# A kernel of conditional layer norms: boundary tokens in half tiles with gathered pair rows, and a sort with one number per token

## The chip, the cores and the metric

The kernel runs on one core of one Trainium2 chip. The metric is the device time of one execution in microseconds (us). Three executions before the change took 1043.15, 1043.70 and 1040.04 us; their median, 1043.15 us, is the time before.

## The reference

Every token has a row x of 512 floats (16 batches of 512 tokens, 8192 tokens) and three indices: a pathway (0 to 499), a compartment c (0 to 4, used for the "cp" and "tm" tables) and a mask m (0 or 1 here; the table "ms" has 3 rows).

```
h = _ln(_ln(x, pw_g[pw], pw_b[pw]), cp_g[c], cp_b[c])
t = _ln(x, tm_g[c], tm_b[c])
s = _ln(x, ms_g[m], ms_b[m])
m_, n_, r_ = x + (a small two-layer network of each batch's condition, with layer norm)   # one row per batch
cat = concatenate(w0*h, w1*t, w2*m_, w3*n_, w4*r_, w5*s)                # 3072 wide
y = _ln(silu(cat @ int_W1 + b1) @ int_W2 + b2, g, b)
out = x + y
```

`w` is a softmax of six numbers, and `_ln(x, g, b)` is (x - mean) * rsqrt(var + 1e-5) * g + b. All is float32. A layer norm's row times g is linear in the normalised row, so t and s together are norm(x) * (w1 * tm_g[c] * W1_t + w5 * ms_g[m] * W1_s) plus a row that depends on (c, m) alone. There are 15 pairs (c, m).

## The kernel before

**Tiles.** The kernel sorts the tokens by pair, so that nearly every tile of 128 sorted tokens has one pair, its primary pair. 64 tiles make 16 windows (`sts`, w = 0 to 15) of four tiles. For a window, x rows are gathered by token (`gather_x`, POOL), their sums taken (`x_sums`, ACT), and three transposed operands made: X (x itself), V (the norm, zero for tokens whose pair isn't the primary one) and H (the pathway and compartment norms). A transposed operand comes about in two steps: DVE turns 32 x 32 blocks (`turn`, L156) into a tile `rot`, and four DMAs issued by SP (`spread_row`, L164) carry a row of it into a tile `cat`, from which TensorE loads its weights. A row of `cat` needs all four gathers of its window, since the turned blocks are interleaved. There is one `rot` and one `cat` tile for each of X, V, H and Z.

Each tile has four products of four chunks of 128: X with wx_ (w2, w3, w4 times their blocks of W1), V with a matrix built for the tile's pair (`s_part` on ACT, `build` on DVE, L190 and L196), H with wh_, and the second layer's Z with w2. The condition networks' part of the first layer and all biases come as one gathered row for each token (`rows_2` in DRAM, `gather_add`).

**Boundary tokens.** A tile in which the sorted list goes from one pair to the next also holds tokens of other pairs. They get their V part apart: for each of the 14 later pairs, the 128 tokens from the tile position where it begins are one extra tile. Four windows e0 to e3 (`ext`) hold them. Their x rows are gathered, normed (`norm_v`) and turned, and for each pair k a matrix is built: `pair_s` (ACT, L597) scales ws by the ms row, `pair` (DVE, L805) adds wt times the tm row. `extra` (PE, L811) is the product, `extra_add` and `extra_end` add a gathered bias row, and `extra_out` writes the 128 rows to rows_2.

**The sort.** Before that, prefix sums of the 15 pairs give each of 8192 tokens its position: row (0 to 127) and tile column (0 to 63). For each of 64 steps (128 tokens, one on each partition) DVE or POOL builds a one-hot row matrix (L563), and DVE (L572) or ACT (L567, L569) builds a matrix with two numbers, the token and its pair with its pathway, at the token's column. A product per step (L574), summed in PSUM, puts them in place. Then the tables of tokens, pathways, compartments and primary pairs follow, by small transposing products (`swap`, L603).

**Order.** Each engine runs its instructions in the order of the program. From window 2 on, a fixed step function writes that order. Before it, the string ORDER names every piece ("gx.e0.1", "pa.4", "lX.1.0") in the order in which it is issued, across engines; a piece in that string is one helper call, and the dictionary `pieces` names the function. All DMAs of SP are issued in one queue, and gathers on POOL's. The first window's products are lX.0.*, lV.0.*, lH.0.*.

Of the kernel before, what the change touches and what calls it, by code (L numbers as in the profile page):

```python
# [8 lines left out]
F32 = mybir.dt.float32  # L9
# [5 lines left out]
P = 128  # L15
# [4 lines left out]
ORDER = """  # L20
    gx.e0.0 gx.e0.1 gx.e0.2 xs.0.0 gx.e0.3 xs.0.2 gx.e1.0 gx.e1.1 xs.0.1 gx.e1.2 xs.0.3 gx.e1.3 pwi xs.e0.0 gh.0.0
    cs cv br2 xe.0 prim cg xs.e0.3 lX.0.0 xp.0 scl cp xm.0 sp.0.0 pk gh.0.1 cn bd.0.0 ct lX.0.1 nv.0.0 lw nv.0.1
    gh.0.2 xs.e0.1 tv.0.0 tv.0.1 nv.0.2 ca lX.0.2 nv.0.3 tv.0.2 sp.0.1 tv.0.3 bd.0.1 sV.0.0 xn.0.0 lX.0.3 xs.e0.2
    f1.0.0 sV.0.1 xn.0.1 xa fp.0.0 cm xe.e0 f1.0.1 sV.0.2 ps.0 xp.e0 xm.e0 fm.0.0 fp.0.1 lV.0.0 sV.0.3 cr fn.0.0
    fm.0.1 f2.0.0 sp.0.2 bd.0.2 gh.0.3 lV.0.1 nv.e0.0 nv.e0.1 tv.e0.0 sp.0.3 gx.e2.0 tv.e0.1 bd.0.3 gx.e2.1 rp.0
    nv.e0.2 nv.e0.3 gx.e2.2 fn.0.1 tv.e0.2 rp.1 xn.0.2 gx.e2.3 tv.e0.3 rc.0 f1.0.2 xs.e1.2 ro.0 lV.0.2 sV.e0.0 rc.1
    f2.0.1 fp.0.2 xs.e1.0 pa.1 xs.e1.1 ro.1 lV.0.3 sV.e0.2 xs.e1.3 fm.0.2 pa.2 fn.0.2 ea.1 xn.0.3 sV.e0.3 ea.2
    f1.0.3 ex.2 xs.e2.2 sV.e0.1 xe.e1 f2.0.2 fp.0.3 xp.e1 fm.0.3 fn.0.3 xm.e1 f2.0.3 nv.e1.0 ea.3 nv.e1.2 ea.4
    tv.e1.0 xs.e2.0 sH.0.0 pa.4 ex.1 gx.e3.0 nv.e1.1 xs.e2.1 gx.e3.1 sH.0.1 tv.e1.1 gx.e3.2 xs.e2.3 ee.1 tv.e1.2
    eo.1 pa.3 nv.e1.3 sH.0.2 ex.3 gx.e3.3 tv.e1.3 sH.0.3 xe.e2 ee.2 xp.e2 lH.0.0 ee.3 ea.5 xm.e2 nv.e2.0 eo.2  # L30
    nv.e2.1 sV.e1.0 gx.1.0 tv.e2.0 tv.e2.1 nv.e2.2 gx.1.1 nv.e2.3 tv.e2.2 ps.1 tv.e2.3 sV.e1.1 gx.1.2 pa.5 gx.1.3
    xs.e3.0 ex.4 sV.e1.2 ea.6 xs.e3.1 pa.6 eo.3 xs.e3.2 ex.5 sV.e2.0 ee.4 xs.e3.3 sV.e2.1 ex.6 gh.1.0 ar pa.7 ea.7
    sV.e1.3 ee.5 xe.e3 pa.8 xp.e3 lH.0.1 sV.e2.2 ee.6 eo.6 ex.8 eo.4 xs.1.0 xs.1.1 xs.1.3 xm.e3 nv.e3.0 nv.e3.1
    tv.e3.0 tv.e3.1 nv.e3.2 eo.5 gh.1.1 gx.2.0 gx.2.1 nv.e3.3 tv.e3.2 sV.e2.3 tv.e3.3 gx.2.2 ex.7 sV.e3.0 ea.8 pa.9
    ea.9 sV.e3.1 lH.0.2 ee.7 eo.7 xs.1.2 ps.2 gx.2.3 xe.1 pa.10 xp.1 sV.e3.2 wm ea.10 ex.10 tx.1.0 tx.1.1 sV.e3.3
    gh.1.2 wl.1 tx.1.2 wl.2 tx.1.3 wl.3 ex.9 xm.1 pa.12 nv.1.0 wl.4 sX.1.0 ee.8 lH.0.3 ee.9 eo.8 pa.11 ea.11 sX.1.2
    ex.11 sX.1.3 ee.10 eo.9 sX.1.1 wl.0 nv.1.1 pa.13 ex.12 tv.1.0 nv.1.2 pa.14 eo.10 ea.12 ex.13 ee.11 tv.1.1 sp.1.0
    eo.11 tv.1.2 bd.1.0 ex.14 ea.13 nv.1.3 sp.1.1 tv.1.3 ea.14 lX.1.0 sV.1.1 ee.12 ee.13 xn.1.0 eo.12 eo.13 ee.14
    lX.1.1 eo.14 sV.1.2 lX.1.2 sV.1.3 ga.0.3 ga.0.0 bd.1.1 sV.1.0 lX.1.3 ga.0.1 f1.1.0 ga.0.2 xn.1.1 xn.1.3 f1.1.1
    ha.0.3 fp.1.0 lV.1.1 hs.0.3 ha.0.0 sh.0.0 fm.1.0 hs.0.0 fp.1.1 fn.1.0 tz.0.0 ha.0.1 sh.0.1 hs.0.1 lV.1.0 ha.0.2  # L40
    sh.0.2 tz.0.1 hs.0.2 tz.0.2 sh.0.3 sp.1.2 tz.0.3 f2.1.0 ga.1.0 sZ.0.1 bd.1.2 sp.1.3 ga.1.1 lV.1.2 sZ.0.2 gh.1.3
    xn.1.2 f1.1.2 sZ.0.0 ga.1.2 l2.0.1 fp.1.2 sZ.0.3 fm.1.1 bd.1.3 fn.1.1 ga.1.3 l2.0.2 f2.1.1 fm.1.2 f1.1.3 gh.2.0
    fn.1.2 l2.0.0 xs.2.0 f2.1.2 xs.2.1 fp.1.3 gh.2.1 fm.1.3 fn.1.3 xs.2.2 f2.1.3 lV.1.3 la.0.0 sH.1.0 xs.2.3 lq.0.0
    tx.2.0 tx.2.1 xe.2 tx.2.2 xp.2 sH.1.1 sp.2.0 la.0.1 l2.0.3 tx.2.3 la.0.2 xm.2 lq.0.1 gh.2.2 bd.2.0 sH.1.2 lq.0.2
    lH.1.0 xn.2.0 xn.2.1 sH.1.3 sh.1.1 sh.1.0 f1.2.0 nv.2.0 nv.2.1 sp.2.1 tv.2.0 lH.1.1 fp.2.0 sX.2.0 tv.2.1 la.0.3
    fm.2.0 f1.2.1 nv.2.2 nv.2.3 sX.2.1 lq.0.3 tv.2.2 fp.2.1 fn.2.0 tv.2.3 lv.0 f2.2.0 lp.0 sX.2.2 ha.1.0 gh.2.3
    hs.1.0 sX.2.3 lH.1.2 lb.0.0 fm.2.1 ha.1.1 fn.2.1 hs.1.1 sh.1.2 f2.2.1 po.0.0 sV.2.0 lH.1.3 tz.1.0 lb.0.1 gx.3.0
    sV.2.1 sh.1.3 sV.2.2 tz.1.1 sV.2.3 ha.1.2 lb.0.2 hs.1.2 po.0.1 gx.3.1
"""
# [3 lines left out]
def kernel(ctx: ExitStack, tc: tile.TileContext, a: dict, out: bass.AP):  # L53

# [339 lines left out]
    for k, nm in enumerate(("idx_c", "idx_m", "idx_pw")):  # L394
        nc.sync.dma_start(idx[:, k, :], a[nm])
# [6 lines left out]
    nc.sync.dma_start(ws, w1_block(5))  # L402
    nc.sync.dma_start(wt, w1_block(1))
    mx = prep.tile([P, 1], F32, name="mx")
    nc.vector.tensor_reduce(mx, aw, AX.X, ALU.max)
    nmx = prep.tile([P, 1], F32, name="nmx")
    nc.vector.tensor_scalar_mul(nmx, mx, -1.0)
    ex = prep.tile([P, 6], F32, name="ex")
    nc.scalar.activation(ex, aw, AF.Exp, bias=nmx)
    stT, w1s = [], []  # L410
    at = 0
    for nm in ("mem", "noi", "res"):
        k = a[nm + "T"].shape[0]
        kk = min(k, P)
        n = k // kk
        t = prep.tile([kk, n, B], F32, name="stT" + nm)
        nc.scalar.dma_start(t, a[nm + "T"].rearrange("(c p) b -> p c b", p=kk))
        stT.append(t)
        t = xbs[2][:kk, at : at + n, :]
        at += n  # L420
        nc.scalar.dma_start(t, a[nm + "_W1"].rearrange("(c p) f -> p c f", p=kk))
        w1s.append(t)
    b1c = prep.tile([P, 4, NC], F32, name="b1c")
    nc.scalar.dma_start(b1c, a["b1c"])
    vr = gp.tile([P, D], F32, tag="cp", name="vr")[:9]
    nc.scalar.dma_start(vr, a["vecs"][:9])
    rb2 = scratch(0, D)
    for s in range(3):
        nc.scalar.dma_start(rb2[s * L : (s + 1) * L], a["vecs"][3 * s].partition_broadcast(L))
    w2s = [xbs[1], xbs[0], w2]  # L430
    for t, nm in zip(w2s, ("mem", "noi", "res")):
        nc.sync.dma_start(t, a[nm + "_W2"].rearrange("(c p) f -> p c f", p=P))
    tabs = scratch(0, 3, NC, L)
    nc.vector.memset(tabs, 0.0)
    for k, (nm, lo, hi) in enumerate((("tm_bT", 0, NR5), ("ms_bT", NR5, NR), ("cp_bT", 0, NR5))):
        nc.sync.dma_start(tabs[:, k, :, lo:hi], a[nm].rearrange("(c p) r -> p c r", p=P))
    w1x = [yb, flat_cat("H", "w1x1"), flat_rot("H", "w1x2")]
# [661 lines left out]
```

## Time and profile before

| what | us |
|---|---|
| median of three runs | 1043.15 |
| the profiled execution: its own time | 1036.91 |
| the profiled execution: its span | 1034.9 |
| PE busy | 987.2 (95% of the span) |
| DVE busy | 876.2 (85%) |
| ACT busy | 572.7 (55%) |
| POOL busy | 570.4 (55%) |
| PE share of the chain that ended last | 82% |

The profile is one execution, taken apart by a hardware profiler; the span runs from the first instruction to the last. PE is TensorE, PEld its weight loads, DVE the vector engine, ACT the scalar engine, POOL GpSimd, SP the engine that only issues DMAs. A float32 product of one chunk of 128 is recorded as two matmuls. The 40-slice table gives each engine's busy share in tenths for slices of 25.9 us. A group row gives a line, engine, operation, output <- input, number; then busy us and mean ns of one; then the idle time of the engine in front of these instructions and what ended it. The TensorE clock granted was 0.988 of full on the mean; four short stretches between 58 and 213 us ran at half.

### The profile page before, as it was taken

What the parts mean: (1) busy time and instruction counts of PE and PEld (TensorE: products, weight loads), DVE (VectorE), ACT (ScalarE), POOL (GpSimd) and SP (SyncE); (2) the same over time, 40 slices, a digit from 0 to 9 for tenths busy, and PEclk for the clock granted to TensorE, in tenths of its full rate; (3) what the DMA queues carried; (4) which work ended last, traced back from release to release, by engine and by line L of the source; (5) the groups of instructions that cost most, each with busy time, mean ns of one, the idle gap of its engine ahead of it and who ended that gap; (6) DMA issues with size and microseconds to landing.
All of it is one profiled execution on the core that took longest, in us unless ns stands there. A gap on an engine that the chain in (4) does not pass through costs nothing.

```text
span 1034.9 us, 11013 instructions
## 1 busy us (share of the span) xinstructions
PE 987.2 (95%) x2523; PEld 447.5 (43%) x2523; DVE 876.2 (85%) x1577; ACT 572.7 (55%) x1153; POOL 570.4 (55%) x573
## 2 busy tenths in 40 slices
PE   5979799899899999999999999999999999999996
PEld 5634244343344444444444444444444444444442
DVE  7978898998889898888888888888898988888844
ACT  3698694483746473646464554647364746474311
POOL 4764661646556564737464646555565647374413
PEclk9989999999999999999999999999999999999998
DMA  9585797566767675857666676767676758677412
GB/s 281 202 264 160 225 287 222 163 178 190 198 195 201 172 224 158 231 161 212 175 195 181 194 191 187 190 198 197 193 200 174 221 155 231 163 215 179 135 51 92
DMA packets 95655, 197.66 MB, mean 191 GB/s; under 512 B 26290, under 2 KB 26290, under 8 KB 95592
## 3 DMA queue, kind: packets, MB, share of 16 engines
q0 software_dynamic: 32096, 108.55, 35.9%
q1 hardware_dynamic: 62230, 87.44, 30.3%
q10 hardware_dynamic: 1266, 0.99, 0.3%
q8 instruction: 21, 0.34, 0.1%
q14 instruction: 42, 0.34, 0.1%
HBM read 104.14 MB, written 21.44 MB: 121 GB/s over the span
## 4 chain that ended last, share of the span: by engine, by line
PE 82%; DVE 5%; DMA 4%; ACT 3%; issue 3%; SPq 1%; POOL 1%; POOLq 0%; DVEq 0%; ACTq 0%
PE p L305 57%; PE p L324 19%; PE pe L811 3%; PE pn L574 1%; SPq L164 1%; DMA xbs<-in_mem_W 1%; DMA out<-yb,tok 1%; PE ph L549 1%; DMA adde<-rows,i_addx 1%; DMA cH<-rH 1%; DVE vs L196 1%; DMA xbs<-in_x,tok_x 1%; DVE pw L289 0%; ACT vs L190 0%; DVE vs L805 0%
## 5 line engine op out<-in xcount | busy, mean ns | idle before, releaser
L305 PE MATMUL p<-vs,cV 128*128 128x512 f32 x504 | 228.4, 597 | 6.7 <-DVE vs L196 6.7
L324 PE MATMUL p<-w,cZ 128*128 128x512 f32 x512 | 228.9, 592 | 0.0
L305 PE MATMUL p<-wx__82,cX 128*128 128x512 f32 x512 | 225.2, 597 | 3.1 <-DVE add L309 2.1
L305 PE MATMUL p<-wh__83,cH 128*128 128x512 f32 x512 | 222.8, 592 | 0.0
L196 DVE SCALAR_TENSOR_TENSOR vs<-wt,sct,vs 128x512 f32<-128x512 f32 x252 | 206.3, 878 | 0.0
L190 ACT ACTIVATE vs<-ws,scs 128x512 f32<-128x512 f32 x252 | 160.7, 707 | 2.6 <-PE pe L811 2.1
L269 POOL TENSOR_TENSOR rsh<-veh,mhalf 128x1 f32<-128x1 f32 x64 | 45.9, 717 | 199.8 <-DVE veh L265 191.1
L305 PEld LDWEIGHTS p<-wx__82,cX 128*128 128x128 f32 x512 | 97.9, 192 | 126.6 <-issue 118.9
L305 PEld LDWEIGHTS p<-vs,cV 128*128 128x128 f32 x504 | 95.5, 191 | 130.9 <-issue 92.3
L324 PEld LDWEIGHTS p<-w,cZ 128*128 128x128 f32 x512 | 97.3, 190 | 122.5 <-issue 122.2
L305 PEld LDWEIGHTS p<-wh__83,cH 128*128 128x128 f32 x512 | 97.3, 190 | 122.5 <-issue 122.2
L276 ACT ACTIVATE pw<-pw,nmh,rsh 128x512 f32<-128x512 f32 x64 | 51.8, 810 | 128.0 <-DVE nmh L147 128.0
L312 ACT ACTIVATE add<-add 128x512 f32<-128x512 f32 x64 | 40.3, 630 | 146.8 <-DVE add L309 141.9
L358 POOL DMA_INDIRECT out<-yb,tok x64 | 68.2, 1066 | 63.8 <-DVE yb L353 26.9
L332 ACT ACTIVATE junk<-yb 128x512 f32<-128x512 f32 x64 | 40.1, 627 | 88.1 <-DVE yb L327 88.0
L130 POOL DMA_INDIRECT add<-rows,i_add x64 | 75.6, 1182 | 22.8 <-issue 9.7
L260 DVE TENSOR_TENSOR pw<-xn,pw 128x512 f32<-128x512 f32 x64 | 44.1, 689 | 48.5 <-ACT xn L237 48.5
L294 POOL TENSOR_TENSOR xbs<-xbs,rows 128x512 f32<-128x512 f32 x64 | 81.5, 1275 | 0.9
L130 POOL DMA_INDIRECT xbs<-in_x,tok x64 | 65.4, 1022 | 24.8 <-issue 17.8
L130 POOL DMA_INDIRECT cp<-cp_rows,i_cp x64 | 68.0, 1062 | 19.5 <-issue 19.2
L130 POOL DMA_INDIRECT pw<-in_pw,i_pw x64 | 64.0, 1000 | 22.2 <-issue 12.7
L237 ACT ACTIVATE xm<-xbs,mnm,mrs 128x512 f32<-128x512 f32 x64 | 48.7, 804 | 39.3 <-DVE rV L156 39.3
(234 smaller groups left out, 1226.1 us busy)
## 6 DMA issues: line engine op xcount, KB each, us to landing
cX<-rX SPq DMA_DIRECT2D x256, 64.0 KB
cV<-rV SPq DMA_DIRECT2D x256, 64.0 KB
cH<-rH SPq DMA_DIRECT2D x256, 64.0 KB
cZ<-rZ SPq DMA_DIRECT2D x256, 64.0 KB
cVe<-rVe SPq DMA_DIRECT2D x64, 64.0 KB
rows<-adde SPq DMA_DIRECT2D x14, 256.0 KB
w1x<-in_int_W SPq DMA_DIRECT2D x2, 1024.0 KB
ws<-in_int_W SPq DMA_DIRECT2D x1, 1024.0 KB
```

The costliest lines, as they stand in the source:

```text
L130: nc.gpsimd.indirect_dma_start(dst, None, table, bass.IndirectOffsetOnAxis(ap=idx, axis=0), **kw)
L190: nc.scalar.activation(v[:, c], ws[:, c], AF.Identity, scale=scs[:, c, g, w : w + 1])
L196: nc.vector.scalar_tensor_tensor(v[:, c], wt[:, c], sct[:, c, g, w : w + 1], v[:, c], ALU.mult, ALU.add)
L237: nc.scalar.activation(t, st["xb"][:, j, :], AF.Identity, bias=st[nm][:, j : j + 1], scale=st[rs][:, j : j + 1])
L260: nc.vector.tensor_mul(pw[:, :D], st.pop(("xn", j)), pw[:, :D])
L269: nc.gpsimd.tensor_tensor(rs, st.pop(("ve", j)), mhalf[:, :1], ALU.pow)
L276: nc.scalar.activation(pw[:, :D], pw[:, :D], AF.Identity, bias=st.pop(("nm", j)), scale=st.pop(("rs", j)))
L294: nc.gpsimd.tensor_add(st["xb"][:, j, :], st["xb"][:, j, :], rows[:, 2, :])
L305: nc.tensor.matmul(st["p1", g], st["c" + blk][:, g, c, :], m[:, c, :], start=(blk == "X" and c == 0), stop=(blk == "H" and c == NC - 1))
L312: nc.scalar.activation(st["add", g], st["add", g], AF.Silu)
L324: nc.tensor.matmul(p2, st["cZ"][:, j, c, :], w2[:, c, :], start=(c == 0), stop=(c == NC - 1))
L358: nc.gpsimd.indirect_dma_start(out_rows, bass.IndirectOffsetOnAxis(ap=tok[:, j, w : w + 1], axis=0), yb[:, j, :], None)
```

## The change

1. **Half tiles.** The primary pair of a tile is now the one at its middle, so a pair's tokens outside its own tiles are at most 64, at one side of a boundary. Two boundaries share one extra tile: seven tiles (`NX = NG // 2`) in two windows e0, e1, not 14 in four.
2. **No pair matrices.** Since one tile holds two pairs, the pair's gain is put on the rows: a DRAM table `pair_rows` (15 rows of tm_g[c], ms_g[m], 4 KB each) is gathered for each token, each half is multiplied by the norm and by w1 or w5, both halves are turned and spread (T and S), and the tile's product is T with wt plus S with ws, eight chunks instead of four.
3. **Sort.** Token and row go as one number, token * 512 + pathway; pairs come by other small products from the 14 places where pairs begin. The one-hot matrices are built in eight batches of eight steps, and the 64-wide column matrix is now the weights (`lhsT`), the 128-wide row matrix the moving side.
4. **Order of loads and pieces.** The three condition blocks of W1 and the first-layer condition weights are loaded first, ws and wt after the positions, the W2s of the condition networks after the sort; the condition networks, tables and the sum wx_ (now in quarters, "wk") became pieces of ORDER, and ORDER as a whole is new. Steps from window 2 on are as before.

```diff
-    rows_2 = dram.tile([NB1 + (NG - 1) * P, D], F32, name="rows_2")
+    NX = NG // 2
+    pair_rows = dram.tile([NG, 2 * D], F32, name="pair_rows")
+    rows_2 = dram.tile([NB1 + NX * P, D], F32, name="rows_2")
...
+    for m in range(NR3):
+        nc.sync.dma_start(pair_rows[m * NR5 : (m + 1) * NR5, :D], a["ct"][:, D:])
+        nc.sync.dma_start(pair_rows[m * NR5 : (m + 1) * NR5, D:], a["ms_g"][m].partition_broadcast(NR5))
+    nc.sync.dma_start(ws, w1_block(5))
+    nc.sync.dma_start(wt, w1_block(1))
...
-    U = 4
+    U = 8
+    places = [m.rearrange("p c f -> p (c f)")[:, : U * (P + NQ)] for m in (*vs, xbs[2])]
+    def one_hots(q0):
+        k = q0 // U
+        oh = places[k % 3]
+        rows_, cols_ = [m.rearrange("p (u n) -> p u n", u=U) for m in (oh[:, : U * P], oh[:, U * P :])]
+        n, m = U - 2, U - 2 - k % 2
+        nc.vector.tensor_tensor(rows_[:, :n], i_col.unsqueeze(1).to_broadcast([P, n, P]),
+                                prow[:, q0 : q0 + n].unsqueeze(2).to_broadcast([P, n, P]), ALU.is_equal)
+        nc.vector.tensor_tensor(cols_[:, :m], i_q.unsqueeze(1).to_broadcast([P, m, NQ]),
+                                pcol[:, q0 : q0 + m].unsqueeze(2).to_broadcast([P, m, NQ]), ALU.is_equal)
+        nc.vector.tensor_tensor(cols_[:, :m], cols_[:, :m],
+                                vals[:, q0 : q0 + m].unsqueeze(2).to_broadcast([P, m, NQ]), ALU.mult)
+        for u in range(n, U):
+            nc.gpsimd.tensor_scalar(rows_[:, u], i_col, prow[:, q0 + u : q0 + u + 1], None, ALU.is_equal)
+        for u in range(m, U):
+            q = q0 + u
+            d2 = dist[:, u % 2]
+            nc.scalar.activation(d2, i_q, AF.Square, bias=pcol[:, q : q + 1], scale=-1.0)
+            nc.scalar.activation(cols_[:, u], d2, AF.Relu, bias=vals[:, q : q + 1], scale=nvals[:, q : q + 1])
         for u in range(U):
             q = q0 + u
...
+            nc.tensor.matmul(pn, cols_[:, u], rows_[:, u], start=(q == 0), stop=(q == NQ - 1))
...
-    ext = [{"w": f"e{e}", "xb": xbs[e % 2], "tok": (tok_x, e)} for e in range(Q)]
-    HOME = "ZXZV"
+    ext = [{"w": f"e{e}", "xb": xbs[e], "tok": (tok_x[:, :, 0], e)} for e in range(2)]
+    HOME = {"e0T": "Z", "e0S": "X", "e1T": "Z", "e1S": "V"}
...
+    def x_block(s, c):
+        nc.vector.scalar_tensor_tensor(wx_[:, c], w1x[s][:, c], wx[:, 2 + s : 3 + s], wx_[:, c], ALU.mult, ALU.add)
...
-    def pair(k):
-        c = k % NR5
-        for i in range(NC):
-            nc.vector.scalar_tensor_tensor(vs[(k + 1) % 2][:, i], wt[:, i], sc[:, i, c : c + 1], bm[:, i],
-                                           ALU.mult, ALU.add)
+    def gather_pair(st, j):
+        tk, e = st["tok"]
+        st["r", j] = r = gp.tile([P, 2 * D], F32, tag="pw", name=f"pr{st['w']}_{j}")
+        gather(r, pair_rows[:, :], tok_x[:, j, 1, e : e + 1])
+    def by_pair(st, j):
+        r, x = st["r", j], st.pop(("xm", j))
+        for v in range(2):
+            m = r[:, v * D : (v + 1) * D]
+            nc.vector.scalar_tensor_tensor(m, x, wx[:, 4 * v + 1 : 4 * v + 2], m, ALU.mult, ALU.mult)
+    def turn_pair(st, j):
+        r = st.pop(("r", j))
+        for v in range(2):
+            turn_to(st, "r" + "TS"[v], HOME[st["w"] + "TS"[v]], j, r[:, v * D : (v + 1) * D])
     def extra(k):
         at_["pe", k] = pe = psum(1, f"pe{k}")
-        for c in range(NC):
-            nc.tensor.matmul(pe, ext[k // Q]["cV"][:, k % Q, c, :], vs[(k + 1) % 2][:, c, :],
-                             start=(c == 0), stop=(c == NC - 1))
+        st = ext[k // Q]
+        for v, m in (("cT", wt), ("cS", ws)):
+            for c in range(NC):
+                nc.tensor.matmul(pe, st[v][:, k % Q, c, :], m[:, c, :],
+                                 start=(v == "cT" and c == 0), stop=(v == "cS" and c == NC - 1))
...
-        nc.sync.dma_start(rows_2[NB1 + (k - 1) * P : NB1 + k * P, :], at_["adde", k])
+        nc.sync.dma_start(rows_2[NB1 + k * P : NB1 + (k + 1) * P, :], at_["adde", k])
```

The start of the boundary tiles in the new ORDER, after window 0's H rows are turned:

```
mt.e0.0 sH.0.1 gr.e0.2 tr.e0.0 gx.e1.2 nv.e0.2 mt.e0.1 sH.0.0 gr.e0.3 lV.0.3 tr.e0.1 nv.e0.3 ea.1 xs.e1.0 mt.e0.2 sH.0.2
gx.e1.3 xs.e1.1 tr.e0.2 lH.0.1 ea.0 mt.e0.3 sH.0.3 xs.e1.2 ea.3 tr.e0.3 ea.2 xs.e1.3 lH.0.0 sT.e0.0 gr.e1.2
xe.e1 xp.e1 sS.e0.0 gr.e1.0 xm.e1 nv.e1.0 lH.0.3 nv.e1.2 gr.e1.1 mt.e1.2 sT.e0.1 gx.1.1 gx.1.0 ex.0 mt.e1.0
```

## The prediction

> **What bounds the kernel now.** I read the 40-slice table first, then a table of stages that I cut myself, then TensorE's instructions in order of time.
>
> ```profile
> PE   5979799899899999999999999999999999999996
> DVE  7978898998889898888888888888898988888844
> ...
> 16.40:41.30 24.90, 24.42 (x144) 21.83 (x144) 23.75 (x88) 19.50 (x56) 19.82 (x32) 1.00 0.85 291
> 57.20:234.50 177.30, 160.47 (x388) 69.80 (x389) 153.28 (x283) 125.20 (x261) 93.05 (x89) 0.96 0.73 214
> ...
> 234.50:296.50 62.00, 56.25 (x129) 23.88 (x129) 54.30 (x89) 32.50 (x63) 36.89 (x35) 1.00 0.69 195
> 330.00:600.00 270.00, 270.00 (x631) 119.39 (x630) 233.65 (x401) 150.86 (x296) 152.44 (x148) 1.00 0.68 191
> ```
>
> In the stage rows the columns are: stretch, length, busy time of PE, PEld, DVE, ACT, POOL, then granted clock, DMA share, GB/s. From 330 us on PE never stops: 631 matmuls in 270 us is 0.43 us each, so one product of four chunks (8 records) is 3.43 us. That part isn't touched; everything is decided before about 297 us. There I see three stages. In the sort (16.4 to 41.3) DVE, POOL and PE are all nearly full. Then PE waits for the first window's X rows. Then 42 products (24 of windows 0 and 1, four of the second layer, 14 boundary tiles) take 177.3 us.
>
> ```profile
> 19.89 21.06 PE L574 MATMUL pn<-oh 128*128 128x128 f32 x128
> 57.22 3.67 PE L305 MATMUL p<-wx__82,cX 128*128 128x512 f32 x8 [1.00 <-DMA cX<-rX]
> 66.64 0.90 PE L755 MATMUL pt<-ident,room 96*128 96x96 f32 x4 [5.75 <-DVE room L750]
> 115.67 5.37 PE L811 MATMUL pe<-vs,cVe 128*128 128x512 f32 x8 [3.11 <-ACT sums L209]
> 174.51 13.90 PE L305 MATMUL p<-wx__82,cX 128*128 128x512 f32 x32
> 234.51 7.03 PE L305 MATMUL p<-wx__82,cX 128*128 128x512 f32 x16
> ```
>
> Here each row is start, length, instruction, and in brackets the idle time before it and who ended it. The first product starts at 57.2, window 1's at 174.5, window 2's at 234.5. 42 x 3.43 = 144.1 us; the small products between (pt 0.7, pb 2.7, pr 5.2 by their distances) are 8.6. So 177.3 - 152.7 = **24.6 us are lost** there: 5.8 before pt, 9.8 in gaps and stretched products among the boundary tiles (102 to 130 us), 4.9 in window 1 (195 to 203), the rest about 3.4 us of half clock (75.8 to 82.6 us). After 234.5 sixteen products need 54.9 of 62.0 us: 7.1 more lost.
>
> **The boundary tiles, part by part.** Their PE work stays: 14 tiles x 4 chunks were 56, 7 tiles x 8 chunks (T with wt, S with ws) are 56. No gain there. What feeds them changes:
>
> ```profile
> L805 DVE SCALAR_TENSOR_TENSOR vs<-wt,sc,yb 128x512 f32<-128x512 f32 x56 | 38.6, 743 | 1.4 <-PE pe L811 0.7
> L597 ACT ACTIVATE yb<-ws,sc 128x512 f32<-128x512 f32 x12 | 8.0, 713 | 4.8 <-PE pb L765 4.2 <-DVE vs L805 0.2
> L819 DVE TENSOR_TENSOR adde<-pe,adde 128x512 f32<-128x512 f32 x14 | 9.5, 682 | 5.6 <-PE pe L811 3.0 <-DMA adde<-rows,i_addx 2.6
> L237 ACT ACTIVATE xme<-xbs,nmx,rsx 128x512 f32<-128x512 f32 x16 | 12.2, 806 | 5.7 <-DVE nmx L227 5.6
> ```
>
> - DVE: the pair matrices go (56 x 0.743 = 41.6), half of the final adds (7 x 0.68 = 4.8); the products with gathered rows come, 8 gathers x 2 halves = 16 of L805's kind and size (11.9). Turns stay 16 (16 x 1 before, 8 x 2 after). Net -34.5.
> - ACT: the 12 scalings go (8.6), 8 norms of 16 (6.4), and 8 of 16 row sums, each 0.625 + 0.723 + two reads of 0.187 + 0.2 = 1.92 (15.4). Net -30.4.
> - POOL: 8 x-gathers (1.09 each) and 7 row gathers (1.03) go, 8 pair gathers come. A pair gather has the form of pw<-in_pw (128 rows of 4 KB, 1.05). Net about -7.5.
> - SP: a boundary tile's rows were 4 transfers, now 8, so 64 in all become 56; the writes to rows_2 fall from 14 to 7. At about 0.62 us an issue, -9.
>
> DVE had 153.3 of 177.3 us; less 34.5 it is 118.8, against 144.1 + 12.9 of PE work. So in the whole stage PE binds, and in-order DVE work ahead of a product shrinks most just where the 9.8 us are lost. DVE and ACT savings are worth nothing themselves; they are worth the stalls they end. These go between nothing (0) and all 9.8; I take half, since the first boundary product now needs all four pair gathers, their products and turns (4 x 4 x 0.7 = 11.2 us of DVE) behind the front of window 0: 5 us remain. In window 1, whose stalls were a DVE backlog (DVE vs L196), 3 of 4.9 remain; of the pt wait 2 of 5.8, because the chain to pt now runs while PE has three X products rather than one; of the clock loss 2. Lost after: 12, that is **-12.6**.
>
> The clock is where I weigh the skill. Trainium skill, "TensorE: Matmul & The Clock Gate", section "What's actually happening": the array falls to half clock after an idle window of about 3.4 us and is released after a busy one. By it all half clock beside products (6.8 us, and two of 3.4 us at 127 and 209) would vanish with the gaps, worth up to 6.8 us. But the half-clock stretch at 75.8 lies eight microseconds into solid products, long after the 5.75 us gap, so the row and the rule don't match in time; I book 1.4.
>
> **The sort.** Before it ran 23.9 us of instructions on DVE (16.4 to 40.3): 64 steps, tensor_scalar and scalar_tensor_tensor 128 wide.
>
> ```profile
> L572 DVE SCALAR_TENSOR_TENSOR oh<-room,room 128x128 f32<-128x128 f32 x50 | 17.6, 380 | 0.0
> L563 POOL TENSOR_SCALAR oh<-room 128x128 f32<-128x128 f32 x32 | 19.9, 637 | 14.6 <-DVE room L534 12.0 <-PE pn L574 2.5
> ...
> L490 DVE TENSOR_TENSOR vs<-grp,i_grp 128x960 f32<-128x960 f32 x1 | 1.2, 1158 | 0.1
> ```
>
> Now 8 batches: 768 + 384 + 384 elements (320 in odd batches). L490 is the same broadcast compare: 960 in 1.158, about 1.04 ns an element and 0.16 fixed, so 0.96 + 0.56 + 0.56 = 2.1 us a batch, 1.95 odd; 8 batches 16.2, and with six small instructions 17.5. PE: 128 records of 0.165 were fed, not bound; 64-column weights can't make it worse, and its 16 records a batch need at most 2.6 at the old pace, of which the fastest 1.8 (0.11 each at 24 to 28 us). ACT: at most three squares and Relus, 3 x 0.77 = 2.3, average 1.9.
>
> Against this speaks the Trainium skill, "SBUF — State Buffer", section "SBUF: two separate sides": a DVE instruction with two SBUF inputs and a GpSimd instruction that reads SBUF lock each other out whole. POOL still builds two rows a batch, and the new DVE instructions are two-input and up to three times as long. By L563's row (0.637) POOL needs 1.3 of 2.1 us and the loop takes 17.5. By the rule each POOL build may sit out a 0.56 to 0.96 us instruction first, near 1.3 us each; with some fifteen small POOL instructions around the first batches that makes about 22 us. The trace backs the rule elsewhere: the gather at 45.55 took 2.55 instead of 0.95 us beside a 2.35 us DVE instruction. I take 19.5.
>
> Ahead of the loop: counts, `tot`, `ends`, `begs`, `base` and half of row_col go, about ten DVE instructions of 0.17 to 0.23, plus the copy of idx: 2 us; idx_c is SP's first transfer instead of second, 0.9. The loop starts at 13.5 instead of 16.4 and ends at 33 instead of 40.3. From there to the gathers was 1.8 us (40.99 to 42.79); one more shift makes 2.0: gathers from 35. They took 6.6 us; beside eight wx_ quarters of some 0.66 us (instead of one whole) between 5 and 9; I take 7.5. Landing 2.6, turn 0.7, spread to first product 4.5, all as before (49.4, 52.0, 52.75, 57.2). First product at **50.3: -7** (45 with no lockout, 53 with all of it).
>
> Loads: SP's order now puts w1x first and the W2s late. Before, 10.9 MB came between 3 and 25 us at up to 400 GB/s; afterwards DMA was idle. Nine small transfers of the changed order sit between w1x and ws; five megabytes at 0.37 MB a microsecond then end near 32 us, before any product wants them. Cost 0, cover some 10 us. The condition products, moved behind the sort, were 7 us of PE in front of it and run while PE waits for the gathers; cost 0. But two condition sums (1.7) and pbt (2.6), which ran before 57.2, now stand behind the first product: **+4.3**.
>
> **Sum.** -7 + 4.3 - 12.6, and of the 7.1 lost after 234.5 I take 2 as gained: -17.3. Own time of the profiled run 1036.9 (span 1034.9 and 2.0 around it) gives 1019.6. The median of the runs is 6.2 higher; as that is what is compared, 1043.15 - 17.3 = 1026, from which I round to **1025**. Ends: -12 + 4.3 - 20.6 - 7.1 = -35 (1008); -4 + 4.3 and nothing else = 0 (1043).
>
> **Rivals.**
> 1. *The loop stays POOL-bound and gathers are stretched*: first product at 56, -1; the rest stands, -11: 1032. For it: 2.55 us gathers. Against it: three batch buffers.
> 2. *Stalls aren't DVE's*: two of the gaps end with a transfer (cVe) or ACT. Then the 12.6 and the last 2 stay: -2.7, 1040.
> 3. *Buffer hand-over, slower*: T of e1 reuses e0's buffer, S of e0 that of X, window 1's X that of S, its V that of e1's S. A first row needs 2.5 us of SP issue and 2 landing; T plus S 7.0. If each of four hand-overs is uncovered, 28 us come, without the stalls' gain: -7 + 4.3 + 28 - 14.6 = +10.7, 1054. It decides where PE has under 7 us between the last reader and the next first one. By the instruction order those covers are 17, 24 and 14 us, and 6.9 for e1's T: one on the edge, hence unlikely.
>
> **Chances.** Forecast 0.70, rivals 0.08, 0.10, 0.12. 0.5% (5 us) is what measurement tells from no change. Faster 0.78, same 0.09, slower 0.13. Range 1007 to 1042.
>
> **What would show it.** Right: last pn product near 33; first X product near 50; window 1's near 159, window 2's near 219; DVE share below 0.75 between them. Wrong: POOL full through the sort with DVE idle; PE waits of over 3 us named cTe, cSe or cX; PE idle after 297 us.

## The result, and the profile after

Five runs of the changed kernel took 1032.66 to 1035.80 us, median 1033.51; five of the kernel before took 1038.82 to 1043.70, median 1042.23. The ratio is 0.9927, with a 95% interval of 0.9903 to 0.9951: 0.7% faster, -8.7 us at the medians. The forecast was -17.3, so half of it is missing. (The changed kernel was measured twice more, on two chips: 0.9948 [0.9929, 0.9968] and 0.9919 [0.9888, 0.9950].)

The page of the profiled execution (1032.66, span 1030.9), busy tenths and granted clock:

```profile
PE   4998999989999999999999999999999999999996
DVE  7678345997888888988888888888888988888844
PEclk9889999999999999999999999999999999999998
```

In the fifth to seventh slice (104 to 181 us) DVE was at 8, 9 and 8 tenths before. Now it is at 3, 4 and 5 there, as predicted, and climbs back to 9 behind it. The same stretches cut again, with the same columns as before:

```profile
13.00:36.60 23.60, 20.75 (x148) 18.15 (x148) 16.06 (x29) 14.54 (x43) 21.54 (x26) 1.00 0.76 255
36.60:58.05 21.45, 19.73 (x180) 13.10 (x179) 13.99 (x36) 14.60 (x42) 12.10 (x11) 0.61 0.74 212
58.05:170.80 112.75, 104.33 (x289) 45.12 (x289) 63.87 (x129) 62.95 (x128) 50.31 (x50) 0.98 0.79 228
170.80:234.40 63.60, 57.04 (x129) 24.80 (x128) 58.20 (x104) 34.21 (x66) 31.48 (x32) 0.97 0.57 157
```

In the sort POOL is busy 21.54 of 23.60 us. In the gather stage TensorE's clock is 0.61. In the boundary stage DVE needs 63.87 of 112.75, in the next one 58.20 of 63.60. TensorE's rows in order of time, with its waits:

```profile
58.05 3.86 PE L278 MATMUL p<-wx__82,cX 128*128 128x512 f32 x8
101.90 8.80 PE L278 MATMUL p<-wh__83,cH 128*128 128x512 f32 x16 [3.78 <-DMA cH<-rH]
112.32 3.67 PE L278 MATMUL p<-wh__83,cH 128*128 128x512 f32 x8 [1.61 <-DMA cH<-rH]
148.83 3.67 PE L877 MATMUL pe<-wt,cTe 128*128 128x512 f32 x8 [1.95 <-DMA cTe<-rTe]
157.02 3.67 PE L877 MATMUL pe<-wt,cTe 128*128 128x512 f32 x8 [1.08 <-DMA cTe<-rTe]
170.82 13.90 PE L278 MATMUL p<-wx__82,cX 128*128 128x512 f32 x32
196.75 10.54 PE L297 MATMUL p<-w,cZ 128*128 128x512 f32 x24 [1.73 <-DMA cZ<-rZ]
218.99 15.59 PE L278 MATMUL p<-wh__83,cH 128*128 128x512 f32 x32 [4.83 <-DMA cH<-rH]
234.42 13.90 PE L278 MATMUL p<-wx__82,cX 128*128 128x512 f32 x32
```

Every wait over 1 us behind the first X product now ends with a transfer, where DVE and ACT ended several before. Behind each of the two long ones TensorE runs at half clock for a while: 16 records take 8.80 instead of 7.1, 32 take 15.59 instead of 13.90, 1.7 us each.

| stage | before | after | change | forecast |
|---|---|---|---|---|
| last pn product (the sort's loop) ends | 40.95 | 36.62 | -4.3 | -7.3 to -8 |
| from there to the first X product | 16.3 | 21.4 | +5.2 | +1 |
| first X product | 57.22 | 58.05 | +0.8 | -7 |
| first X to window 2's X | 177.3 | 176.4 | -0.9 | +4.3 - 12.6 = -8.3 |
| window 2's X to window 3's | 62.0 | 55.8 | -6.2 | -2 |
| window 3's X to the end | 738.4 | 740.7 | +2.3 | 0 |
| sum (profiled runs) | | | -4.0 | -17.3 |

The profiled run of the kernel before lay 5.3 us under its median, that of the changed one 0.9 under its own; that is why the profiles differ by 4.0 and the medians by 8.7. A second caution: two more profiles of the changed kernel have the first X product at 58.11 and 59.20 and window 3's X at 288.7 and 291.3, but one experiment profiled twice (f2 and i1 below) differs by 4.4 and 6.4 us in these places. So a shift of a stage by one or two microseconds between single profiles proves little; what follows rests on what a wait is and on how long an operation takes, and totals on their intervals.

### The profile page after: what moved, and what is told of

Read it like the earlier page. It is cut to its first block, busy times and chain, and to the rows that moved or that the text cites. A ratio compares the mean times of both kernels' runs of the same rounds, so it can differ in the third digit from the quotient of the medians.

```text
span 1030.9 us, 10853 instructions
## 1 busy us (share of the span) xinstructions
PE 987.5 (96%) x2573; PEld 447.4 (43%) x2573; DVE 826.8 (80%) x1442; ACT 545.6 (53%) x1096; POOL 566.3 (55%) x580
## 4 chain that ended last, share of the span: by engine, by line
PE 65%; DVE 13%; DMA 6%; SPq 4%; issue 3%; ACT 2%; POOL 1%; POOLq 0%; DVEq 0%; ACTq 0%
PE p L278 47%; PE p L297 15%; DVE vs L169 5%; SPq L137 4%; PE pe L877 4%; DMA cH<-rH 3%; DVE pw L262 1%; DVE sth L108 1%; DVE pw L234 1%; DVE pw L233 1%; DMA cV<-rV 1%; DMA cSe<-rSe 1%; DVE rV L129 1%; DMA out<-yb,tok 1%; DMA cTe<-rTe 1%
## 5 line engine op out<-in xcount | busy, mean ns | idle before, releaser
L278 PE MATMUL p<-wh__83,cH 128*128 128x512 f32 x512 | 226.2, 600 | 10.2 <-DMA cH<-rH 10.2
L103 POOL DMA_INDIRECT xbs<-in_x,tok x64 | 65.0, 1015 | 23.6 <-issue 17.9
L103 POOL DMA_INDIRECT cp<-cp_rows,i_cp x64 | 65.1, 1017 | 19.5 <-issue 18.9
```

The source lines that it names most:

```text
L103: nc.gpsimd.indirect_dma_start(dst, None, table, bass.IndirectOffsetOnAxis(ap=idx, axis=0), **kw)
L278: nc.tensor.matmul(st["p1", g], st["c" + blk][:, g, c, :], m[:, c, :], start=(blk == "X" and c == 0), stop=(blk == "H" and c == NC - 1))
```

## The experiments

All eighteen start from the changed kernel; two, h0 and i0, are that kernel again. Except for work that is added, and named, they compute the same. Given are the ratio to the kernel before and its interval; for the changed kernel these are 0.9919 to 0.9948.

### The sort: two limits side by side

**e1**: no one-hot rows on POOL.

```diff
-        n, m = U - 2, U - 2 - k % 2
+        n, m = U, U - 2 - k % 2
```

> The changed kernel, but all eight row one-hots of a batch are built on DVE (one instruction of 1024 elements instead of 768) and none on POOL; what is computed stays the same. Theory (the loop waits for POOL, whose builds stretch beside DVE's two-input instructions): DVE's batch grows by 0.27 us to 2.2 to 2.4, the last pn product ends near 32.5 to 33.5 instead of 36.6, and the first X product comes some 3 us sooner; total -3 (about 1030). Rival (DVE itself, or PE's pace at half clock, bounds the loop): last pn product at 38 to 39, total +2.

Ratio 0.9901 [0.9865, 0.9937]. The last pn product ended at 34.98, 1.6 sooner, only half of what was expected, and the first X product stayed at 57.68: neither the theory nor the rival. TensorE's rows of this kernel:

```profile
15.01 3.68 PE L553 MATMUL pn<-vs 128*64 128x128 f32 x16 [7.24 <-DVE bi L566]
19.98 3.52 PE L553 MATMUL pn<-vs 128*64 128x128 f32 x16
23.33 1.91 PE L553 MATMUL pn<-xbs 128*64 128x128 f32 x16
```

The first two batches take 3.68 and 3.52 us, the third, of the same 16 records, 1.91. TensorE had been idle for 7.24 us. So with POOL away a second limit appears: TensorE at the slow pace. The kernel before was slow there as well, though the condition products ran in front of its loop. Its rows, in the columns of the stage tables, show 20 records in 4.1 us and then 36 in 4.0:

```profile
19.90:24.00 4.10, 4.10 (x20) 4.10 (x20) 3.66 (x15) 2.24 (x9) 1.83 (x4) 1.00 1.13 304
24.00:28.00 4.00, 4.00 (x36) 3.95 (x35) 4.00 (x14) 3.67 (x12) 4.00 (x8) 1.00 1.04 379
```

The clock column reads 1.00 in both rows, but the trace's first clock record, of full clock, lies at 24.3 us in the kernel before and in the changed kernel, and at 23.2 in e1. Ahead of it nothing is recorded, and the column shows 1.00 all the same. What the change did is to start the loop at 15.0 instead of 19.9, so that more of it lies in the slow stretch.

**f1** and **f2**: warm TensorE, with POOL's rows and without.

```diff
+    warm = ps_1.tile([P, P], F32, tag="p1", name="warm")
+    for _ in range(20):
+        nc.tensor.matmul(warm, ident, ident, start=True, stop=True)
     for q0 in range(0, NQ, U):
         one_hots(q0)
```

> The changed kernel with twenty products of the identity with itself (128x128, about 6.5 us of TensorE work that nothing needs) put on TensorE ahead of the sort's first batch, where it is idle for 7.2 us. Theory (TensorE starts the sort cold: its first two batches take 3.6 us where later ones take 1.8, since the condition products that ran ahead of the sort before now run behind it): the first batches take 1.8 to 2 us, but POOL still holds the loop, last pn product at 34 to 35.5 instead of 36.6; total -1 to -2. Rival (the long first batches are fed late by POOL, not slow): first batches still 3.5, last pn product at 36.3 to 37, total 0 to +1.

> The same warming products, and all row one-hots on DVE, none on POOL. Theory (the loop has two limits, the cold TensorE and POOL, and either alone hides the other's removal): last pn product at 32 to 33.5, that is 3 to 4.5 us sooner than the changed kernel, where no POOL rows alone gave 1.6. Rival (DVE's own 2.4 us a batch or the small products bound it): 34 to 35.5.

f1: 0.9955 [0.9935, 0.9975]. The second batch's 12 fed records took 1.52 us, but then TensorE waited 4.65 us for POOL's rows, fell back to half clock from 22.5 to 29.4, and needed 3.56 us for the third batch. The loop ended at 39.28, which is a miss for theory and rival: warming alone gained nothing. f2: 0.9866 [0.9838, 0.9895], with:

```profile
15.18 1.96 PE L553 MATMUL pn<-vs 128*64 128x128 f32 x16 [1.38 <-DVE bi L566]
17.92 1.96 PE L553 MATMUL pn<-vs 128*64 128x128 f32 x16
19.89 1.96 PE L553 MATMUL pn<-xbs 128*64 128x128 f32 x16
```

Each batch of 16 takes 1.96 or little more, the loop ends at 32.86, where the forecast had put it, and the first X product comes at 53.22. Yet window 2's X came at 233.42, only 1.0 sooner than in the changed kernel: behind the first X product the time was lost again (below).

**f5**: the condition products back in front of the sort.

```diff
+    ph_all = ps_2.tile([P, 3, NC, B], F32, tag="p2", name="ph")
+    for s in (2, 1, 0):
...
+                nc.tensor.matmul(at_ph[:, c, :], w1s[s][:, k, c * P : (c + 1) * P], stT[s][:, k, :],
...
     for q0 in range(0, NQ, U):
```

> The changed kernel with the condition networks' first layer (32 small products, one PSUM tile) ahead of the sort, where it stood in the kernel before; its Silu stays behind the sort. Theory (moving these products behind the sort cost time twice: TensorE started the sort cold, and the chain Silu, second layer, sums, norm, pt, which window 0's front waits for, came 6 us later): second-layer products begin near 40 to 43 instead of 49.5, first H product of window 0 at 95 to 98 instead of 101.9, window 2's X at 227 to 231 instead of 234.4, total -4 to -7. Rival (they are hidden behind the gathers, as the forecast said): total within 1.5.

Ratio 0.9966 [0.9946, 0.9987]: a miss.

```profile
15.89 1.85 PE L616 MATMUL ph<-stTres,w 32*128 32x16 f32 x8 [8.12 <-DMA w<-in_res_W]
...
23.01 3.68 PE L553 MATMUL pn<-vs 128*64 128x128 f32 x16
27.67 1.96 PE L553 MATMUL pn<-vs 128*64 128x128 f32 x16
```

TensorE waited until 15.9 for the weights and then ran these products at the slow pace for 7.1 us; the loop began at 23.0 and ended at 41.1. Its first batch was slow all the same, and full clock came at 27.1. So these products, of 16 columns each, do not bring TensorE to full pace as the 20 warming products of 128 columns do (full clock at 10.6 in f2, 2.9 us after they began): their place is not what made the changed loop start slow. What the lateness of the weights cost here, and what the slow pace did, this run does not separate.

**i0** and **i1**: the changed kernel and f2 again, on one chip.

> The changed kernel beside i1, five rounds. Expected 1033 to 1035, ratio 0.990 to 0.996 to the kernel before.

> f2_warm_no_pool (warming products ahead of the sort, no row one-hots on POOL) beside the changed kernel on one chip. Theory (the sort's two limits carry most of the shortfall): last pn product near 33, first X product near 53.5, total 4.5 to 7 us below i0, ratio 0.985 to 0.989. Rival (front gains are taken back behind the boundary tiles, as window 2's X, sooner by 1 us only, suggests): 0 to 2 us below i0.

i0: 1035.06, 0.9919 [0.9888, 0.9950]. i1: 1032.93, 0.9902 [0.9878, 0.9926]: 2.1 us less, nearer to the rival, and not told apart from no difference. In i1's profile the loop ended at 35.19 instead of 32.86: a small product waited for POOL (1.47 us), and the two batches behind it took 5.37 instead of 3.9, with half clock from 25.2 to 28.6. Of the seven profiles with f2's sort, three ended the loop at 32.9, one at 33.4 and three at 35.1 to 35.2; nine with the changed sort ended it at 36.4 to 38.5. e1's single 34.98 lies within f2's range, so what warming adds once POOL is away is shown by the batches' lengths and not by every loop's end. POOL's small instructions in the two profiles of the same code, f2's first:

```profile
19.43 2.37 POOL L573 TENSOR_SCALAR wh__83<-wh__83,half 14x64 f32<-14x64 f32 x2
```
```profile
20.23 4.17 POOL L573 TENSOR_SCALAR wh__83<-wh__83,half 14x64 f32<-14x64 f32 x2
```

An instruction of 14 x 64 takes 0.44 to 0.47 when DVE does one-input work or none, and here 1.2 to 2.1 on the mean beside DVE's compares. The rule that the forecast weighed (Trainium skill, "SBUF — State Buffer", section "SBUF: two separate sides": the two lock each other out whole) agrees with these rows and those of the changed kernel, where L493 took 0.44 and L495, of the same form, 1.64. How often it hits differs from run to run.

### The way to the first X product: two limits again

**e2**: TensorE's order. `h2.2` and `eh.1` move behind `lX.0.0`.

```diff
-xs.0.3 se cg gh.0.2 he.1 h2.2 xe.0 scl sX.0.1 eh.1 sp.0.0 bd.0.0 xp.0 lX.0.0 sX.0.3
+xs.0.3 se cg gh.0.2 he.1 xe.0 scl sX.0.1 sp.0.0 bd.0.0 xp.0 lX.0.0 h2.2 eh.1 sX.0.3
```

> The changed kernel with one edit of its order: h2.2 and eh.1 (a condition sum of 1.9 us and its evaluation) stand behind window 0's first X product instead of in front of it. Theory (PE's in-order small products at half clock delay the first X product, whose rows had landed near 54): first X product at 55.5 to 56.2 instead of 58.05, the 1.9 us come back after it at full clock as about 1.0; total -1 to -1.5. Rival (the rows landed only just before 58, PE's small work merely filled a wait): first X product stays at 57.5 to 58.1, total 0 to +1.

Ratio 0.9984 [0.9965, 1.0003]. The first X product came at 58.38 and waited 3.59 us for its rows: the rival's answer. The total was worse by some 4 to 7 us, which neither expected. Window 0's first H product moved from 101.90 to 107.91; I read this as the condition sums coming later, and with them the norm and DVE's in-order front of window 0.

**f3**: the indices of window 0's six pathway and c-row gathers are made later (`pwi` behind `cg`, the gathers behind it).

> The changed kernel with an order edit on DVE: the indices of window 0's pathway and c-row gathers (pwi) are made behind the last X turn and the small table work (51.5 instead of 45.5), so that these six gathers, 2.3 MB, reach the DMA queues behind the first X spreads; tok_x also stands behind the last turn. Theory (the X rows' spread took 8.7 us from first issue to first product where it took 4.4 before, because those gathers share the DMA engines with it): first X product at 54 to 56 instead of 58.05. What follows may lose some of it, since window 0's front gets its rows later; total -2 to +2. Rival (the spread is slow by itself, or TensorE's small products hold it): first X product at 57 to 58.5.

Ratio 0.9968 [0.9950, 0.9985]. First X product at 57.25, within the rival's range; but now without a wait: TensorE's small products, most of them at half clock, reached to 57.3. Behind its own loop's end (37.52) the product came after 19.7 us, where three profiles of the changed kernel have 20.8 to 22.8.

**h1**: both at once; the gathers stand behind `xp.0` on POOL.

```diff
-... pwi wk.1.2 gh.0.0 cv sz ... xs.0.2 gh.0.1 tk ... cg gh.0.2 he.1 h2.2 xe.0 scl sX.0.1 eh.1 sp.0.0 bd.0.0 xp.0 lX.0.0
+... pwi wk.1.2 cv sz ... xs.0.2 tk ... cg he.1 xe.0 scl sX.0.1 sp.0.0 bd.0.0 xp.0 gh.0.0 gh.0.1 gh.0.2 lX.0.0 h2.2 eh.1
```

> The changed kernel with both limits of the first X product moved: window 0's six pathway and c-row gathers stand behind the power for the row norms (xp.0) on POOL, so they reach the DMA queues at about 55 instead of 46, and h2.2 and eh.1 stand behind the product on TensorE. Theory (two limits side by side, each hiding the other): from the last pn product to the first X product 17 to 18.5 us instead of 21.4. Rival (the spread is slow by itself): 20.5 to 21.5. The total may still rise, as the condition sums come later (e2 lost 6 us that way).

First X product 18.1 us behind the loop instead of 21.4: the theory. The spread and the product, first in the changed kernel, then in e2, then in h1 (issues on SP's queue; TensorE):

```profile
49.39 12.56 SPq L137 DMA_DIRECT2D cX<-rX  x16
...
58.05 3.86 PE L278 MATMUL p<-wx__82,cX 128*128 128x512 f32 x8
```
```profile
58.38 5.23 PE L278 MATMUL p<-wx__82,cX 128*128 128x512 f32 x8 [3.59 <-DMA cX<-rX]
```
```profile
50.55 10.11 SPq L137 DMA_DIRECT2D cX<-rX  x16
...
54.58 4.39 PE L278 MATMUL p<-wx__82,cX 128*128 128x512 f32 x8 [0.26 <-DMA cX<-rX]
```

From first issue to product 8.7 us became 4.0 (4.4 in the kernel before). The DMA engines' share in 51 to 54 and 54 to 57 us fell from 0.87 and 1.04 to 0.36 and 0.41. In the changed kernel TensorE comes free only at 58.0, so 8.7 is not the spread alone. The clean pair is e2 and h1, in both of which TensorE waits for the rows and which differ by the gathers' place alone: 7.4 us (first issue at 51.03) against 4.0. So the six gathers, 2.3 MB, which the changed order lets POOL issue straight behind the x gathers, took the engines from the spread. The total of h1 is 0.9964 [0.9947, 0.9981], no gain: window 1's X came at 177.7 instead of 170.8. Window 0's front had its rows and its condition sums later, which I take for the cause.

**h0** and **h2**: the changed kernel again, and f2 with the gathers behind `xp.0`.

> The changed kernel itself, for comparison with h1 to h3 on one chip. Expected within 2.5 us of its first runs beside the kernel before (ratio 0.990 to 0.995), last pn product at 36.5 to 38.5.

> f2_warm_no_pool with the six gathers behind xp.0, TensorE's order left as it is. In f2 the X rows were the later limit by 0.96 us, so the first X product can come at most about 1 us sooner: 52.2 to 52.8 if the loop ends at 32.9. Theory (the gains of the front survive only as far as the next wait that has its own clock): window 2's X at 232 to 234, total within 2 of f2. Rival: the whole microsecond, or more, comes through to the end.

h0: 0.9948 [0.9929, 0.9968]. h2: 0.9944 [0.9922, 0.9967], beside h0 on one chip: no gain. First X product at 54.04 (20.6 us behind its loop, 20.4 in f2) and window 2's X at 238.7, both worse than expected: with the gathers alone moved TensorE was the limit, and window 0's front had its rows late.

### Was DVE's saved time worth anything?

**e4**: DVE filled again with work that nothing needs.

```diff
     def extra(k):
...
+        for _ in range(2):
+            for i in range(NC):
+                nc.vector.scalar_tensor_tensor(yb[:, i], wt[:, i], wx[:, 1:2], ws[:, i], ALU.mult, ALU.add)
```

> The changed kernel with DVE filled again: eight scalar_tensor_tensor of 128x512 that nothing needs follow each boundary product, 56 in all, about 42 us, as many as the pair matrices that the change removed. Theory (DVE's saved 34.5 us turned almost wholly into DVE waiting behind the boundary tiles): window 2's X at most 5 us later, total 0 to +5. Rival (the saved DVE time is what the change's gain of 8.7 us is made of): window 2's X 12 to 25 us later, total +10 or more, back to or above the kernel before.

My theory fell, and the rival held. Ratio 1.0031 [1.0009, 1.0052], 8 to 12 us slower than the changed kernel and slower than the kernel before; window 2's X at 246.61, 12.2 later. TensorE's row in e4:

```profile
157.60 5.12 PE L880 MATMUL pe<-wt,cTe 128*128 128x512 f32 x8 [11.11 <-DMA cTe<-rTe]
```

So 42 us of DVE work, put in this place, are worth about 12, and what hides the rest is DVE's waiting. As the whole change gained 8.7, other parts of it must cost some of that again; this run does not say which.

### Where the front's gain goes: e1's first rows

In f2 TensorE waits 5.01 us for e1's first T rows, 1.95 in the changed kernel. A buffer hand-over (rival 3) or bandwidth? The row in f2:

```profile
146.69 5.59 PE L880 MATMUL pe<-wt,cTe 128*128 128x512 f32 x8 [5.01 <-DMA cTe<-rTe]
```

**e3**: S of e1 in H's buffer, `lH.0.2` moved up behind `lH.0.3`. **g3** and **g4**: e1's halves change buffers, with f2's sort and with the changed one.

```diff
-    HOME = {"e0T": "Z", "e0S": "X", "e1T": "Z", "e1S": "V"}
+    HOME = {"e0T": "Z", "e0S": "X", "e1T": "Z", "e1S": "H"}
...
+    HOME = {"e0T": "Z", "e0S": "X", "e1T": "V", "e1S": "Z"}
```

> The changed kernel, but the S rows of e1 take the rotating buffer of H instead of V's, and window 0's last H product is moved up behind the one before it. Theory (the buffer hand-over holds DVE: window 1's first V turn waits 13.6 us at 159.9 for e1's S rows to leave the buffer): that wait falls under 2 us, window 1's X near 169, window 2's X at 229 to 231 instead of 234.4, total -4. Rival (DVE's wait is slack, since window 1 has other holds, such as the write and re-reading of the last boundary rows): window 2's X at 233.5 to 235, total within 1.5 of the changed kernel.

> f2_warm_no_pool, and e1's halves change buffers: T takes V's, which has been free since 95, S takes that of e0's T; e1's three T spreads move up in SP's queue accordingly. Theory (buffer hand-over: e1's T had to wait until TensorE had read the last T of e0, then for SP's issue and the landing, 5 to 7 us against a cover of one H product): the 5.0 us wait goes, and DVE's 13 us wait for the V buffer shrinks to under 6; window 1's X at 163 to 165 instead of 169.3, window 2's X at 226 to 230 instead of 233.4; total -4 to -6 against f2. Rival (bandwidth or DVE's own lateness): the wait stays over 3, total within 1.5 of f2.

> The changed kernel with the swap of buffers alone (sort as changed, cold). Theory (hand-over): its waits of 1.95 and 1.08 us for T rows go, DVE's 13.6 us wait shrinks, window 2's X at 229 to 231 instead of 234.4, total -3 to -5 against the changed kernel. Rival: within 1.5.

e3: 0.9968 [0.9948, 0.9989], a miss; DVE's 13.6 us wait was gone, but without the H product as cover TensorE waited 4.75 us for e1's T, and window 2's X came at 240.6, 2.0 of this lateness being there at the first X product. g3: 0.9867 [0.9817, 0.9917], as f2; g4: 0.9933 [0.9910, 0.9955], as the changed kernel, with window 2's X at 240.9, another miss. In g3 T comes without a wait, and S waits instead:

```profile
142.31 3.60 PE L880 MATMUL pe<-wt,cTe 128*128 128x512 f32 x8
149.65 5.37 PE L880 MATMUL pe<-ws,cSe 128*128 128x512 f32 x8 [3.75 <-DMA cSe<-rSe]
```

So the swap moves the wait from T to S, the half that now takes over the buffer. That fits a hand-over and a lack of bandwidth alike. (g3 and g4, which differ by the sort's two edits alone, ran on one chip: 1028.84 and 1035.02.)

**g1**: window 1's pathway and c-row gathers held back on POOL by copying their indices again later. **g5**: this and the swap. **h3**: g5 and h2's edit.

```diff
+    def again():
+        for i in (i_pw, i_cp):
+            nc.vector.tensor_copy(i[:, :, 1], i[:, :, 1])
```

> f2_warm_no_pool, and window 1's first three pathway and c-row gathers (2.3 MB) are held back on POOL until its V scales are made (about 141 instead of 132), by copying their indices once more on DVE there. Theory (contention: e1's first T rows were issued at 134.8 and reached TensorE only at 146.7, because these gathers filled the DMA engines just then): TensorE's wait of 5.0 us at e1's first product falls to 0 to 2, its half clock behind it goes, window 1's X at 164 to 166 instead of 169.3; total -3 to -5 against f2. Rival (the rows wait for the queue and the buffer, not for bandwidth): the wait stays at 4 to 5, total within 1.5 of f2 or worse, as window 1's front gets its rows later.

> f2_warm_no_pool with both edits. If hand-over and contention each delay e1's rows, this is the fastest, 1 to 2 us below the better of the two; if the swap has taken the wait away already, holding the gathers back only costs, 0 to +2 against g3.

> h2 with the buffers of e1 swapped and window 1's gathers held back (g5). If the separate gains add, first X product near 52.5, window 2's X 176.3 later as in g5, near 229, total -4 against f2 and near 0.983 of the kernel before. Rival (each gain is taken back by a later wait): 232 to 234, total as f2.

g1: 0.9885 [0.9840, 0.9931], g5: 0.9902 [0.9871, 0.9932], h3: 0.9913 [0.9887, 0.9939]; none gained on f2. But the wait named in the expectation is gone in g1, and another takes its place (TensorE, and in the last row DVE):

```profile
146.73 3.60 PE L884 MATMUL pe<-wt,cTe 128*128 128x512 f32 x8
150.17 3.60 PE L884 MATMUL pe<-ws,cSe 128*128 128x512 f32 x8
...
174.91 7.59 PE L278 MATMUL p<-wx__82,cX 128*128 128x512 f32 x11 [3.98 <-DMA cX<-rX]
```
```profile
164.22 0.69 DVE L892 TENSOR_TENSOR adde<-pe,adde 128x512 f32<-128x512 f32 x1 [6.53 <-DMA adde<-rows,i_addx]
```

From the first X product to window 1's X g1 takes 111.1 us, g5 109.6, f2 116.1 and the changed kernel 112.8. To window 2's X it is 179.7, 176.3, 180.2 and 176.4. In g1 T keeps its buffer, and yet from T's first issue to the product the time falls from 11.9 us (f2) to 6.7, with a DMA share of 0.42 instead of 0.93. So at e1 bandwidth is the limit: the gathers and the spreads want the same DMA engines. The new wait in g1 has another cause. There the gather of a boundary tile's bias rows (`adde`) stands behind the moved gathers on POOL, at 156.9 where the changed kernel has it at 149.6; DVE's final add waits for it, and SP's queue stands 7.5 us for that add before it issues window 1's next X rows, at 165.3. The DMA share is only 0.4 to 0.6 from then on, so it is order, not bandwidth.

One wait is in the changed kernel and in all eighteen experiments, but not in the kernel before: 4.3 to 5.6 us for window 1's H rows, near 219 in the changed kernel. In the changed kernel DVE has no idle time above 0.4 us between 187.5 and 212.1, when the last turn for the first H row ends:

```profile
193.44 7.92 DVE L169 SCALAR_TENSOR_TENSOR vs<-wt,sct,vs 128x512 f32<-128x512 f32 x8
201.29 0.68 DVE L233 TENSOR_TENSOR pw<-xn,pw 128x512 f32<-128x512 f32 x1
...
211.38 0.71 DVE L129 STREAM_TRANSPOSE rH<-pw 128x512 f32<-128x512 f32 x1
```

It idles for some 40 us between 102 and 171, waiting for pair rows, turns and boundary products, and is full from there on. I read this as a place where gains of the front can end; an earlier front of window 1 (f1.1.2 and f1.1.3 ahead of its builds) wasn't tried, so it stays open.

## Why the prediction was wrong, step by step

- **The sort** (loop of 19.5 us from 13.5, end near 33): wrong by 3.6. DVE's instructions cost what the broadcast compare gave (0.96, 0.55, 0.56), but the last product came at 36.62. The step that failed is "PE: 128 records of 0.165 were fed, not bound", with at most 2.6 us a batch: TensorE began at half pace, 3.5 us and more for each of the first two batches instead of 1.9. The mean of 0.165 hid that the old loop, too, ran slow until 24.3; the forecast took its pace from 24 to 28 us. The other half is POOL, busy 21.5 of 23.6. Each hides part of the other (e1 -1.6, f1 nothing, f2 -1.4 to -3.8 in seven profiles). Rival 1 had POOL; the slow start was in no case of the forecast.
- **From the loop to the first X product** (17.3): 21.4. Gathers and turns came out within about a microsecond each: 8.4 us from the loop to the last gather's end where 9.5 were forecast, 4.3 from there to the end of the last turn where 3.3 were. The failed term is "spread to first product 4.5, as before": 8.7, since the order moved six gathers beside it (7.4 with them, 4.0 without, in e2 and h1). "Condition products ... cost 0" failed beside it: with the gathers moved (f3) TensorE's small products alone held the first X product until 57.3.
- **Small products behind the first X product** (+4.3): about right; by the distances of their starts 1.0 for two sums and 2.6 for pbt.
- **Lost time between first X and window 2's X** (24.6 to 12): it fell to about 20 (176.4 - 152.7 - 3.6). The waits in the list above make 15.0, the half clock behind two of them 3.4. The forecast's mechanism holds in part: DVE's busy time came out (122.1 us where 118.8 were announced), e4 shows that DVE's time is worth something there, and the gaps among e0's tiles (115.8 to 143.3) are all gone. The remainders were mis-sized: 5.4 at window 0's H rows, just ahead of the boundary tiles (5 had been left for these); none at pt (2); 6.6 at window 1's Z and H where the forecast has "3 of 4.9 remain"; 3.4 of half clock (2); and 3.0 at e1's T, for which the sum had nothing. Window 1's first X product came at 170.8 where 159 had been announced, window 2's at 234.4 for 219.
- **After 234.5** (-2): -6.2 up to window 3's X; undersized, and why is open. The +2.3 behind it lies in code that wasn't changed, and other profiles have 738.9 to 743.9 there; I make nothing of it.
- **The clock**: the forecast held the rule of the Trainium skill ("TensorE: Matmul & The Clock Gate", section "What's actually happening": half clock after an idle window of about 3.4 us) to be at odds with the row, as the half-clock stretch lay at 75.8. That was misread: its clock times (75.8, 127, 209), and those in the section on the profile before, lie 10.5 us too late against the rows of instructions. The kernel before has the stretch from 65 to 72, at and behind the gap of 60.9 to 66.6, and the others at 48.2, 116.5 and 198.4:

```profile
65.00:72.00 7.00, 5.36 (x10) 2.77 (x11) 6.93 (x14) 6.93 (x15) 5.99 (x4) 0.52 0.97 341
```

  For this long wait rule and row agree. As a threshold 3.4 us isn't sharp here: behind the first X product, in the twenty profiles, every wait of 3.6 us or more was followed by half clock, none under 2.1 was, and between the two some were. The stretch lasts 3.4 us or, after most waits over 4.3, 6.8 (10.2 after e4's wait of 11.1), so the price of a long wait is the wait plus 1.7 us or up to twice that. In the changed kernel there is one that no wait explains: half clock holds from 41.4 to 58.4, over most of the small products ahead of the first X product, though TensorE was recorded busy in 4.3 of the 4.7 us before it. Like the condition products, these are narrow; what sets it off wasn't tested.
- **The sum**: it added the front's -7 to gains further on. Whether a front's gain arrives differs from version to version. f2 won 4.8 at the first X product and 1.0 at window 2's; h2 won 4.1 on h0 at the first and lost 5.0 at window 2's, with equal medians; h1 won 3.5 at the first and lost 7 at window 1's. But g3 won 6.3 on g4 at the first X product, 7.6 at window 2's and 6.2 in the medians, on one chip. These are single profiles, and what decides it is open.
- **The rivals**: rival 1 (1032, POOL-bound loop) came nearest in time, in part by luck: POOL was one of two limits, but gathers were quick and the spread was slow, and what it kept of the forecast behind the first product came out at -7.1 us instead of -10.3. Rival 2 (stalls aren't DVE's) is against e4 and the vanished gaps. Rival 3 showed at the very edge that the text named, e1's T, with 1.95 us; g1 says bandwidth there, not the buffer.

No version beats the changed kernel beyond doubt. f2 is the best candidate, at 0.9866 and 0.9902; with the swap of buffers (g3) it has 0.9867.

## What to carry to other kernels

Before the mean time of an instruction is carried over to a loop that starts earlier, cut the old loop into short stretches: a slow start can hide in a mean, and the work in front of it may not be what ends it. Where an experiment that takes away one limit gives nothing, take away the second one with it before the theory is dropped (POOL and the slow start; gathers and small products). And don't simply add a gain at the front to gains further on: follow it to the next wait, and ask whether those rows come by a chain of their own.

## What the hardware showed that I had not expected

- The same 16 records took 3.68 us after 7.2 us of idleness and 1.96 after warming, while the granted clock reads 1.00 in both stretches. The trace's first clock record lies at 23.2 us in the one kernel and at 10.6 in the other; ahead of it the pace shows in the lengths of the products, not in that column.
- 7.1 us of products of 16 columns each did not bring TensorE to full pace: the 16 records behind them took 3.68 us (f5). Products of 128 columns did so within 2.9 us (f2) and 4.3 us (f1).
- Gathers from POOL nearly double the time of SP's spread, and the wait names the spread's rows alone: 7.4 against 4.0 us from first issue to product (e2, h1), with a DMA share of 0.92 against 0.33.
- One POOL instruction of 14 x 64 took between 0.44 and about 2.1 us, the long times beside DVE's compares; the loop of the same code ended at 32.86 and at 35.19.
